# Values of a halo-attention layer: once per pixel through DRAM, in place of once per window

## The chip, the cores and the metric

The kernel runs on one core of a Trainium2 chip, as one program. The metric is the device time in microseconds, the median of several runs. The core has a matmul engine (TensorE, PE in the profile, with PEld for its loads of the stationary operand), a vector engine (DVE), a scalar engine (ACT), a general engine (POOL), a queue engine that issues most transfers (SP), and 16 DMA engines that all transfers share.

## What is computed

The input x is (2, 128, 256, 256) in fp32: two images of 128 channels. Two layers follow each other, each added to its input:

```
x = x + L0(groupnorm(x))        # halo attention
x = x + L1(groupnorm(x))        # convolutions
```

Layer 0, cut to what matters here:

```python
qkv = jnp.einsum('bchw,oc->bohw', x, W_qkv)
q, k, v = jnp.split(qkv, 3, axis=1)
q = ... # blocks of 8 x 8 pixels
k = unfold_windows(k)     # windows of 12 x 12 pixels, 8 apart: neighbours overlap by 4
v = unfold_windows(v)
attn = jnp.einsum('bnd,bmd->bnm', q * SCALE, k)          # 4 heads of 32
attn = attn + rel_pos_emb(q, rel_height, rel_width) + FIXED_MASK
out = jnp.einsum('bnm,bmd->bnd', softmax(attn), v)
out = ... # back to pixels
return jnp.einsum('bchw,oc->bohw', out, W_out)
```

The mask is minus infinity at every even relative row or column, so a query sees only keys of the other parity of row and of column. A block therefore falls into four classes of row parity r and column parity c, with 16 queries and 6 x 6 keys each. Layer 1 is a 5x1 convolution, a 3x1 depthwise one, a dilated 1x3 product with grouped weights, and their product. The change doesn't touch it.

## The kernel before

A strip is 8 rows of pixels, with its halo 12 rows. A unit u is a strip k and a row parity r, u = 2k + r; two images of 32 strips make 128 units. The normalised pixels of a strip lie in `xn[k % 2]`, a tile of [channel, row parity, column parity, XC = 131 columns j, 6 rows i]. One block needs 6 columns and neighbours start 4 apart, so with 6 rows in a column a pair of neighbouring blocks (10 columns, 60 keys, taken as 64) is one contiguous run, and the next pair starts 48 elements further. There are NPAIR = 16 pairs in a strip.

The values: keys must lie on partitions for the product with the attention weights, so the pixels of a pair are the stationary operand and the value weights stream past it. Every pair is done by itself; where the runs of two pairs overlap, the pixels are computed again. The two column parities fill the lower and the upper 64 partitions.

```python
vt = cst.tile([P, NPAIR, HEADS, 2, 33], F32, tag="f_vt", name="f_vt")   # 33rd column: ones
...
        def values(u, j):
            k, r = divmod(u, 2)
            xt = xn[k % 2].rearrange("p r c j i -> p r c (j i)")
            bank = []

            def part(n):
                if n == 0:
                    bank.append(ps_pj.tile([P, 512], F32, tag="pj", name=f"f_pv_{u}_{j}"))
                pv = bank[0]
                for c in range(2):
                    o = 48 * (4 * j + n)
                    nc.tensor.matmul(
                        pv[64 * c : 64 * c + 64, P * n : P * n + P], xt[:, r, c, o : o + 64], wvT,
                        start=True, stop=True,
                    )
                if n == 3:
                    for c in range(2):
                        rows = slice(64 * c, 64 * c + 64)
                        (nc.vector.tensor_copy if c else nc.scalar.copy)(
                            vt[rows, 4 * j : 4 * j + 4, :, c, 0:32],
                            pv[rows].rearrange("p (n h d) -> p n h d", n=4, h=HEADS),
                        )

            return [lambda n=n: part(n) for n in range(4)]
```

The vector engine and the scalar engine copy each bank into `vt`; the 33rd column of each head is 1 in the rows of its own column parity, so the sum of the attention weights comes out beside the product. `attend` uses `vt`:

```python
        def attend(u):
            p = pts.pop(u)
            on = wk.tile([P, 2, NPAIR, 32], F32, tag="on", name=f"f_on_{u}", bufs=1)
            k, r = divmod(u, 2)
            if r == 0:
                rcs[0] = wk.tile([P, 2, NPAIR, 2, 1], F32, tag="rc", name=f"f_rc_{k}")
            for lo, hi in ((0, 6), (6, 11), (11, NPAIR)):
                bank = ps_pj.tile([P, 512], F32, tag="pj", name=f"f_o_{u}_{lo}")
                po = bank[:, 0 : 66 * (hi - lo)].rearrange("p (n c d) -> p n c d", c=2, d=33)
                for n in range(lo, hi):
                    for h in range(HEADS):
                        nc.tensor.matmul(
                            po[32 * h : 32 * h + 32, n - lo], p[:, h, 32 * n : 32 * n + 32],
                            vt[:, n, h], start=True, stop=True,
                        )

                rc = rcs[0][:, r, lo:hi]
                nc.vector.reciprocal(rc, po[:, :, :, 32:33])
                nc.vector.tensor_tensor(
                    on[:, :, lo:hi].rearrange("p c n d -> p n c d"), po[:, :, :, 0:32],
                    rc.to_broadcast([P, hi - lo, 2, 32]), ALU.mult,
                )
        ...
```

The bias and score matmuls stand in `biases(u)` (line 360) and `scores(u, half)` (line 374), which end in the exponentials (line 382); the keys in `keys(u)` (line 278), the queries in `queries(u)` (line 297), the coefficients of the biases in `coefficients(k, t2)` (line 315), the output projection in `project(u)` (line 424), which adds the input rows and writes the result to DRAM. The order on TensorE is set by hand, on the other engines it is left to a scheduler:

```python
        load_rows(0)
        load_rows(1)
        with tc.manual_schedule(engines={PE}):
            normalise(0)
            emit(keys(0) + queries(0))
            for t2 in range(4):
                emit(coefficients(0, t2))
            for u in range(NU + 1):
                k, r = divmod(u, 2)
                b, s = divmod(k, NS)
                if u == NU:
                    project(u - 1)
                    break
                more = k + 1 < NB * NS
                if r == 0:
                    if k + 2 < NB * NS:
                        load_rows(k + 2)
                    if more:
                        normalise(k + 1)
                if b + 1 < NB and s + 1 < NS:
                    stats_chunk(b + 1, 2 * s + r)
                    if u < 2:
                        stats_chunk(b + 1, 2 * NS - 2 + u)

                biases(u)
                scores(u, 0)
                for j in range(4):
                    emit(values(u, j))
                scores(u, 1)
                if u + 1 < NU:
                    emit(keys(u + 1))
                if u > 0:
                    project(u - 1)
                attend(u)
                if more:
                    emit(coefficients(k + 1, 2 * r) + coefficients(k + 1, 2 * r + 1))
                if u + 1 < NU:
                    emit(queries(u + 1))
                del qs[u]
```

Rows are loaded by `load_rows(k)`, 10 rows of 256 pixels into a pool of four buffers, and normalised by `normalise(k)` (line 260); `stats_chunk` loads rows of the next image for its statistics (line 109). Ahead of all this the statistics of the first image are taken from 32 loads of 1 MB.

Of the kernel before, what the change touches and what calls it, by code (L numbers as in the profile page):

```python
# [9 lines left out]
F32 = mybir.dt.float32  # L10
# [8 lines left out]
P = 128  # L19
W = 256  # L20
HEADS = 4
# [118 lines left out]
        return mean, rstd  # L140


def attention_fast(tc, io, x1_d, norm, st_x, st_y, tags, ends):

    nc = tc.nc
    x = io["x"]
# [3 lines left out]
    with ExitStack() as l0:  # L150
# [34 lines left out]
        for c in range(2):  # L185
            nc.gpsimd.memset(vt[64 * c : 64 * c + 64, :, :, c, 32:33], 1.0)
        nc.gpsimd.memset(wb, 0.0)

        with ExitStack() as setup:
            sp = setup.enter_context(tc.tile_pool(name="f_setup", bufs=6))  # L190


            wq_nat = sp.tile([P, P], F32, tag="wq_nat", name="f_wq_nat", bufs=1)
            nc.sync.dma_start(wq_nat, io["w_q"])
            relT = sp.tile([P, 2 * NREL], F32, tag="relT", name="f_relT", bufs=1)
            nc.sync.dma_start(relT, io["relT"])
            g_rel = sp.tile([P, HEADS, 2 * NREL], F32, tag="g_rel", name="f_g_rel", bufs=1)
            for h in range(HEADS):
                pg = ps_pj.tile([P, 512], F32, tag="pj", name=f"f_pg_{h}")
                nc.tensor.matmul(  # L200
                    pg[:, : 2 * NREL], wq_nat[32 * h : 32 * h + 32, :],
                    relT[32 * h : 32 * h + 32, :], start=True, stop=True,
                )
# [123 lines left out]

            return [lambda t=t: part(t) for t in range(4)]

        def values(u, j):  # L330
            k, r = divmod(u, 2)
            xt = xn[k % 2].rearrange("p r c j i -> p r c (j i)")
            bank = []

            def part(n):
                if n == 0:
                    bank.append(ps_pj.tile([P, 512], F32, tag="pj", name=f"f_pv_{u}_{j}"))
                pv = bank[0]
                for c in range(2):
                    o = 48 * (4 * j + n)  # L340
                    nc.tensor.matmul(  # L341
                        pv[64 * c : 64 * c + 64, P * n : P * n + P], xt[:, r, c, o : o + 64], wvT,
                        start=True, stop=True,
                    )
                if n == 3:
                    for c in range(2):
                        rows = slice(64 * c, 64 * c + 64)
                        (nc.vector.tensor_copy if c else nc.scalar.copy)(  # L348
                            vt[rows, 4 * j : 4 * j + 4, :, c, 0:32],
                            pv[rows].rearrange("p (n h d) -> p n h d", n=4, h=HEADS),  # L350
                        )

            return [lambda n=n: part(n) for n in range(4)]

        def biases(u):
            k, r = divmod(u, 2)
# [27 lines left out]
        def attend(u):  # L384
# [9 lines left out]
                    for h in range(HEADS):  # L394
                        nc.tensor.matmul(  # L395
                            po[32 * h : 32 * h + 32, n - lo], p[:, h, 32 * n : 32 * n + 32],
                            vt[:, n, h], start=True, stop=True,
                        )

                rc = rcs[0][:, r, lo:hi]  # L400
# [209 lines left out]
def kernel_body(tc, io, out):  # L610
# [3 lines left out]
    with ExitStack() as ctx:  # L614
# [13 lines left out]
        attention_fast(tc, io, x1_d, norm, st_x, st_y, tags, ends)  # L628
# [572 lines left out]
```

## Time and profile before

| | |
|---|---|
| time, median of 3 | 4054.06 us (4048.38 to 4065.66) |
| span of the profiled run | 4070.9 us, mean granted TensorE clock 0.977 |
| first matmul of the first image's normalisation | 93.5 us |
| first and last bias matmuls of layer 0 | 111.5 us, 2645.8 us |
| matmuls of the values (line 341) | 8192 records, 521.0 us |
| their copies to `vt` (line 348) | DVE 512 x 694 ns, ACT 512 x 583 ns |
| DMA over the span | 362.10 MB, mean 89 GB/s |

A row of the profile's table of groups names the line, the engine, the operation, the tile written and the tiles read, the shapes, and the count, then the busy time in total, the mean of one, and the idle time of the engine ahead of it with what ended it. An fp32 matmul of the source appears as two records of TensorE, each with its load. The ends of matmuls are modelled: where one follows another, the distance of their starts says more than their length. In the 40 slices each digit is a tenth of the slice.

### The profile page before, as it was taken

What the parts mean: (1) busy time and instruction counts of PE and PEld (TensorE: products, weight loads), DVE (VectorE), ACT (ScalarE), POOL (GpSimd) and SP (SyncE); (2) the same over time, 40 slices, a digit from 0 to 9 for tenths busy, and PEclk for the clock granted to TensorE, in tenths of its full rate; (3) what the DMA queues carried; (4) which work ended last, traced back from release to release, by engine and by line L of the source; (5) the groups of instructions that cost most, each with busy time, mean ns of one, the idle gap of its engine ahead of it and who ended that gap; (6) DMA issues with size and microseconds to landing.
All of it is one profiled execution on the core that took longest, in us unless ns stands there. A gap on an engine that the chain in (4) does not pass through costs nothing. (4 is left out here: it accounts for less than half of the span.)

```text
span 4070.9 us, 144840 instructions
## 1 busy us (share of the span) xinstructions
PE 3641.6 (89%) x67638; PEld 2218.5 (54%) x67638; DVE 2272.4 (56%) x3377; ACT 1384.2 (34%) x2237; POOL 1084.9 (27%) x914
## 2 busy tenths in 40 slices
PE   0778988889989888988988989989999999999997
PEld 0556666666666666666666666643333334333333
DVE  8777656565655565656556565544444444444443
ACT  0333444444444444444444444422222222222221
POOL 1212222122222222212222122123333333333333
PEclk9999999999999999999999999989999999999998
DMA  9562212212212121221212211122222222222221
GB/s 377 190 198 81 68 60 68 68 55 68 72 56 65 55 68 55 73 68 55 68 55 73 68 55 65 34 92 104 97 90 104 104 93 96 101 103 104 90 97 70
DMA packets 71315, 362.10 MB, mean 89 GB/s; under 512 B 8496, under 2 KB 9136, under 8 KB 50224
## 3 DMA queue, kind: packets, MB, share of 16 engines
q1 hardware_dynamic: 43056, 218.49, 16.3%
q0 software_dynamic: 27648, 134.23, 8.4%
q8 instruction: 533, 8.73, 0.9%
q14 instruction: 78, 0.64, 0.1%
HBM read 218.48 MB, written 134.22 MB: 87 GB/s over the span
## 5 line engine op out<-in xcount | busy, mean ns | idle before, releaser
L570 PE MATMUL a<-xm,w 128*128 128x512 f32 (+1 forms) x2560 | 1129.8, 594 | 0.0
L570 PEld LDWEIGHTS a<-xm,w 128*128 128x128 f32 x2560 | 471.6, 188 | 654.5 <-issue 653.8
L589 DVE SCALAR_TENSOR_TENSOR t<-t,w,t 128x2048 f32<-128x2048 f32 x128 | 323.2, 2525 | 752.7 <-ACT t L574 752.6
L348 DVE COPY f_vt<-f_pv 64x512 f32<-64x512 f32 x512 | 354.1, 694 | 656.1 <-ACT f_vt L348 653.6
L348 ACT COPY f_vt<-f_pv 64x512 f32<-64x512 f32 x512 | 298.5, 583 | 756.2 <-PE f_pv L341 756.2
L341 PE MATMUL f_pv<-f_wqkvT,f_xn 128*64 128x128 f32 x8192 | 521.0, 286 | 29.6 <-issue 29.2
L374 PEld LDWEIGHTS f_s<-f_q,f_kt 32*64 32x64 f32 x32768 | 405.0, 134 | 194.0 <-issue 185.4
L374 PE MATMUL f_s<-f_q,f_kt 32*64 32x32 f32 x32768 | 411.6, 227 | 106.9 <-issue 106.6
L341 PEld LDWEIGHTS f_pv<-f_wqkvT,f_xn 128*64 128x64 f32 x8192 | 482.3, 144 | 43.1 <-issue 36.4
L574 ACT COPY t<-a 128x512 f32<-128x512 f32 (+1 forms) x256 | 149.6, 585 | 901.7 <-PE a L570 886.4
L268 POOL COPY f_xq<-f_xn 128x512 f32<-128x512 f32 x256 | 350.8, 1407 | 330.3 <-DVE f_xn L260 295.4
L321 ACT ACTIVATE f_cf<-f_pa,f_keep 128x256 f32<-128x256 f32 x256 | 207.1, 809 | 535.2 <-PE f_pa L315 534.5
L425 DVE TENSOR_TENSOR f_x<-f_py,f_raw 128x512 f32<-128x512 f32 x256 | 176.9, 693 | 263.3 <-PE f_py L424 260.7
L382 ACT ACTIVATE f_p<-f_s 128x512 f32<-128x512 f32 x512 | 265.4, 602 | 131.8 <-PE f_s L374 131.8
L286 POOL COPY f_kt<-f_kt 128x524 f32<-128x524 f32 x124 | 83.0, 669 | 841.5 <-ACT f_kt L281 841.5
L395 PEld LDWEIGHTS f_o<-f_vt,f_p 128*32 128x32 f32 x16384 | 241.4, 110 | 107.5 <-ACT f_kt L281 77.4
L315 PE MATMUL f_pa<-f_xq,f_wb 128*128 128x128 f32 x2048 | 276.5, 286 | 17.8 <-DVE f_on L402 14.6
L278 PE MATMUL f_pk<-f_xn,f_wqkvT 128*128 128x512 f32 (+1 forms) x528 | 277.0, 647 | 15.6 <-DVE f_vt L348 10.5
L395 PE MATMUL f_o<-f_vt,f_p 128*32 128x66 f32 x16384 | 263.6, 222 | 9.0 <-DVE f_x L425 9.0
L315 PEld LDWEIGHTS f_pa<-f_xq,f_wb 128*128 128x128 f32 x2048 | 248.7, 192 | 33.8 <-issue 14.7
L253 POOL COPY f_xn<-f_xn 128x1048 f32<-128x1048 f32 x62 | 71.1, 1146 | 732.2 <-PE f_pv L341 732.2
L424 PE MATMUL f_py<-f_ot,f_woT 128*128 128x512 f32 x512 | 246.3, 603 | 4.0 <-DVE f_ot L409 2.5
(103 smaller groups left out, 3601.4 us busy)
## 6 DMA issues: line engine op xcount, KB each, us to landing
f_raw<-in_x SPq DMA_DIRECT2D x62, 1280.0 KB, 7.0
f_x<-f_x POOLq DMA_DIRECT2D x128, 512.0 KB, 5.0
out<-y POOLq DMA_DIRECT2D x64, 1024.0 KB, 4.5
raw<-f_x SPq DMA_DIRECT2D x64, 640.0 KB, 4.2
f_sx<-in_x SPq DMA_DIRECT2D x32, 1024.0 KB, 12.4
f_sx<-in_x SPq DMA_DIRECT2D x64, 512.0 KB, 3.9
raw<-f_x SPq DMA_DIRECT2D x62, 384.0 KB, 4.7
f_raw<-in_x SPq DMA_DIRECT2D x2, 1024.0 KB, 5.6
```

The source lines that it names most:

```text
L268: nc.gpsimd.tensor_copy(xq[:, t2], by_place[:, t2])
L278: nc.tensor.matmul(pk[:, : n * P], wkT, xt[:, r, c, 1:129, lo:hi], start=True, stop=True)
L315: nc.tensor.matmul(pa[:, P * t1 : P * t1 + P], wb[:, t2, t1].rearrange("p h x -> p (h x)"), xq[:, t2, t1].rearrange("p a m -> p (a m)"), s ...
L321: nc.scalar.activation(cf[:, 0, t2], by_e[:, 0], AF.Identity, bias=keep[:, 1:2], scale=keep[:, 0:1])
L341: nc.tensor.matmul(pv[64 * c : 64 * c + 64, P * n : P * n + P], xt[:, r, c, o : o + 64], wvT, start=True, stop=True,)
L348: (nc.vector.tensor_copy if c else nc.scalar.copy)(vt[rows, 4 * j : 4 * j + 4, :, c, 0:32], pv[rows].rearrange("p (n h d) -> p n h d", n=4 ...
L374: nc.tensor.matmul(sc[h][64 * c : 64 * c + 64, 32 * n : 32 * n + 32], keys_k[rows, c, 48 * n : 48 * n + 64], qs[u][rows, c, 32 * n : 32 * ...
L382: nc.scalar.activation(pts[u][:, h], sc[h], AF.Exp)
L395: nc.tensor.matmul(po[32 * h : 32 * h + 32, n - lo], p[:, h, 32 * n : 32 * n + 32], vt[:, n, h], start=True, stop=True,)
L424: nc.tensor.matmul(py, woT, ots.pop((u, c)), start=True, stop=True)
L570: nc.tensor.matmul(pa[:, : n * W], w1[:, tap, :], xt[:, j - 2 + tap : j - 2 + tap + n, 2 : 2 + W], start=tap == 0, stop=tap == 4,)
L589: nc.vector.scalar_tensor_tensor(t3, t1[:, tap : tap + 8, :], w3[:, tap : tap + 1], t3, ALU.mult, ALU.add)
```

## The change

The values are computed once for every pixel. For a unit, each of the four new cells i of a column is a matmul of its own: 128 columns j of the pixel tile, 6 elements apart, are the stationary operand, and the values come out with columns on the partitions. One copy for each column parity takes a bank to `vx`, whose 33rd column holds ones from the start. From there a transfer writes them to a DRAM tile `v_d[r][k % 2]` of [column parity, 131 columns, 6 cells, 4 x 33], in which the order of memory is the order of keys; a second transfer writes the two cells that the next strip shares into that strip's tile. `gather(u)` then reads the 64 keys of every pair from DRAM into `vt`, one transfer for each column parity, 64 partitions by 16 pairs by 132 numbers. The edge columns of the DRAM tiles are filled once, with zeros and ones.

What this is for: the matmuls of the values use all 128 columns of the array, repeat nothing, and are copied out of PSUM in full height; the overlap is made by the transfers.

The values of unit u+1 are made in unit u, between the halves of the scores, and gathered after `attend(u)`. `vt` changes the order of its axes, with the column parity ahead of the head, and stays one tile with one buffer. The row loads move from the first unit of a strip to the second, and their pool goes from four buffers to three. Cut to its core:

```diff
-        vt = cst.tile([P, NPAIR, HEADS, 2, 33], F32, tag="f_vt", name="f_vt")
+        vt = cst.tile([P, NPAIR, 2, HEADS, 33], F32, tag="f_vt", name="f_vt")
+
+        vx = [cst.tile([P, 2, 4, HEADS, 33], F32, tag=f"f_vx{i}", name=f"f_vx{i}") for i in range(2)]
+        vx0 = cst.tile([P, 2, 2, HEADS, 33], F32, tag="f_vtop", name="f_vtop")
+
+        v_d = [
+            [dram.tile([2, XC, 6, HEADS * 33], F32, tag=f"f_v{r}{i}", name=f"f_v{r}{i}") for i in range(2)]
+            for r in range(2)
+        ]
...
         with ExitStack() as setup:
+            pad = ...tile([6, HEADS, 33], F32, tag="f_pad", name="f_pad")
+            nc.gpsimd.memset(pad, 0.0)
+            nc.gpsimd.memset(pad[:, :, 32:33], 1.0)
+            for r in range(2):
+                for i in range(2):
+                    for c in range(2):
+                        for j in (0, XC - 2, XC - 1):
+                            nc.sync.dma_start(v_d[r][i][c, j], pad.rearrange("p h d -> p (h d)"))
...
-        rawp = l0.enter_context(tc.tile_pool(name="f_raw", bufs=4))
+        rawp = l0.enter_context(tc.tile_pool(name="f_raw", bufs=3))
...
-        def values(u, j):
...
+        def values(u):
+
             k, r = divmod(u, 2)
...
+            s = k % NS
+            parts = [(0, vx0)] if s == 0 else []
+            for lo, t in parts + [(2, vx[u % 2])]:
+                n = 4 if lo else 2
+                banks = [ps_pj.tile([P, 512], F32, tag="pj", name=f"f_pv_{u}_{lo}_{c}") for c in range(2)]
                 for c in range(2):
...
+                    for i in range(n):
+                        nc.tensor.matmul(
+                            banks[c][:, P * i : P * i + P], xn[k % 2][:, r, c, 1:129, lo + i], wvT,
+                            start=True, stop=True,
                         )
...
+                    (nc.scalar.copy if c else nc.vector.tensor_copy)(
+                        t[:, c, :, :, 0:32],
+                        banks[c][:, : n * P].rearrange("p (i h d) -> p i h d", i=n, h=HEADS),
+                    )
+                nc.sync.dma_start(
+                    v_d[r][k % 2][:, 1:129, lo : lo + n].rearrange("c j i x -> j c (i x)"),
+                    t.rearrange("p c i h d -> p c (i h d)"),
+                )
+            if s + 1 < NS:
+                nc.sync.dma_start(
+                    v_d[r][(k + 1) % 2][:, 1:129, 0:2].rearrange("c j i x -> j c (i x)"),
+                    vx[u % 2][:, :, 2:4].rearrange("p c i h d -> p c (i h d)"),
+                )
+
+        def gather(u):
+
+            k, r = divmod(u, 2)
+            for c in range(2):
+                flat = v_d[r][k % 2][c].rearrange("j i x -> (j i) x")
+                src = bass.AP(
+                    tensor=flat.tensor, offset=flat.offset,
+                    ap=[[HEADS * 33, 64], [48 * HEADS * 33, NPAIR], [1, HEADS * 33]],
+                )
+                nc.sync.dma_start(
+                    vt[64 * c : 64 * c + 64, :, c].rearrange("p n h d -> p n (h d)"), src
+                )
...
-                            vt[:, n, h], start=True, stop=True,
+                            vt[:, n, :, h], start=True, stop=True,
...
             emit(keys(0) + queries(0))
+            values(0)
+            gather(0)
...
-                if r == 0:
-                    if k + 2 < NB * NS:
-                        load_rows(k + 2)
-                    if more:
-                        normalise(k + 1)
+                if r == 0 and more:
+                    normalise(k + 1)
+                if r == 1 and k + 2 < NB * NS:
+                    load_rows(k + 2)
...
                 scores(u, 0)
-                for j in range(4):
-                    emit(values(u, j))
+                if u + 1 < NU:
+                    values(u + 1)
                 scores(u, 1)
...
                 attend(u)
+                if u + 1 < NU:
+                    gather(u + 1)
```

More of the change, by code (lines that the diff above doesn't have):

```diff
@@ L140, in group, with attention_fast @@
         return mean, rstd
-def attention_fast(tc, io, x1_d, norm, st_x, st_y, tags, ends):
+def attention_fast(tc, io, x1_d, norm, st_x, st_y, tags, ends, dram):
     nc = tc.nc
@@ L184, in attention_fast @@
         nc.gpsimd.memset(vt, 0.0)
-        for c in range(2):
-            nc.gpsimd.memset(vt[64 * c : 64 * c + 64, :, :, c, 32:33], 1.0)
+        for i in range(2):
+            nc.gpsimd.memset(vx[i], 1.0)
+        nc.gpsimd.memset(vx0, 1.0)
         nc.gpsimd.memset(wb, 0.0)
         with ExitStack() as setup:
+            pad = setup.enter_context(tc.tile_pool(name="f_pad", bufs=1)).tile(
+                [6, HEADS, 33], F32, tag="f_pad", name="f_pad"
+            )
+            nc.gpsimd.memset(pad, 0.0)
+            nc.gpsimd.memset(pad[:, :, 32:33], 1.0)
+            for r in range(2):
+                for i in range(2):
+                    for c in range(2):
+                        for j in (0, XC - 2, XC - 1):
+                            nc.sync.dma_start(v_d[r][i][c, j], pad.rearrange("p h d -> p (h d)"))
             sp = setup.enter_context(tc.tile_pool(name="f_setup", bufs=6))
@@ L328, in coefficients @@
             return [lambda t=t: part(t) for t in range(4)]
-        def values(u, j):
+        def values(u):
             k, r = divmod(u, 2)
[L332 to L338, printed above, removed]
-                for c in range(2):
[L340 to L343, printed above, removed]
-                    )
[L345 to L353, printed above, removed]
+            s = k % NS
[3 more added lines that the diff above has]
+                banks = [ps_pj.tile([P, 512], F32, tag="pj", name=f"f_pv_{u}_{lo}_{c}") for c in range(2)]
+                for c in range(2):
+                    for i in range(n):
[6 more added lines that the diff above has]
+                        banks[c][:, : n * P].rearrange("p (i h d) -> p i h d", i=n, h=HEADS),
+                    )
+                nc.sync.dma_start(
[7 more added lines that the diff above has]
+                )
@@ new lines, in gather @@
+        def gather(u):
[8 more added lines that the diff above has]
+                    vt[64 * c : 64 * c + 64, :, c].rearrange("p n h d -> p n (h d)"), src
+                )
@@ L627, in kernel_body @@
         ends = glob.tile([P, NB * NS], F32, tag="f_ends", name="f_ends")
-        attention_fast(tc, io, x1_d, norm, st_x, st_y, tags, ends)
+        attention_fast(tc, io, x1_d, norm, st_x, st_y, tags, ends, dram)
         good = in_range(tc, glob, ends)
```

## The prediction

> **What bounds the kernel now.** I read the page first, for the busy shares and the 40 slices, then a table of busy time for the stretch of layer 0 alone, then TensorE's timeline over two units of layer 0, then what TensorE waited for there. The shares and slices of the page:
>
> ```profile
> PE 3641.6 (89%) x67638; PEld 2218.5 (54%) x67638; DVE 2272.4 (56%) x3377; ACT 1384.2 (34%) x2237; POOL 1084.9 (27%) x914
> ...
> PE   0778988889989888988988989989999999999997
> ...
> DMA  9562212212212121221212211122222222222221
> ```
>
> TensorE is the busiest engine from the third slice on. The change touches layer 0 alone: from 111.5 us (first bias matmuls) to 2645.8 us (last ones) the timeline counts 127 unit periods, so one of the 128 units takes 19.95 us on average. Busy time in that stretch:
>
> ```profile
> 104.00:2656.00 2552.00, 2256.02 (x62811) 1670.50 (x62810) 1564.07 (x2741) 1055.12 (x1797) 584.03 (x570) 0.97 0.22 73
> ```
>
> The columns are PE, PEld, DVE, ACT, POOL, granted clock, DMA share, GB/s. PE 88%, DVE 61%, ACT 41%, DMA 22%: TensorE bounds this stretch, the transfers have room. One unit on TensorE (start, length, engine, line, operation, count; brackets give idle time before it):
>
> ```profile
> 1023.23 1.12 PE L360 MATMUL f_s<-f_cf,f_hot 32*64 32x512 f32 x16 [1.48 <-DVE f_cf L324]
> 1024.14 1.53 PE L374 MATMUL f_s<-f_q,f_kt 32*64 32x32 f32 x128
> 1025.60 3.81 PE L341 MATMUL f_pv<-f_wqkvT,f_xn 128*64 128x128 f32 x64
> 1029.34 1.28 PE L374 MATMUL f_s<-f_q,f_kt 32*64 32x32 f32 x105
> 1031.35 0.43 PE L374 MATMUL f_s<-f_q,f_kt 32*64 32x32 f32 x23 [0.73 <-issue]
> 1031.71 2.02 PE L278 MATMUL f_pk<-f_xn,f_wqkvT 128*128 128x512 f32 x4
> 1033.58 1.88 PE L424 MATMUL f_py<-f_ot,f_woT 128*128 128x512 f32 x4
> 1035.38 2.05 PE L395 MATMUL f_o<-f_vt,f_p 128*32 128x66 f32 x128
> 1037.36 2.15 PE L315 MATMUL f_pa<-f_xq,f_wb 128*128 128x128 f32 x16
> 1039.34 1.88 PE L297 MATMUL f_pq<-f_xn,f_wq_s 128*128 128x512 f32 x4
> ```
>
> One source matmul in fp32 is two records. The values of line 341 occupy TensorE from 1025.60 to 1029.34, **3.74 us**; the coefficients of line 315, 16 records of a full 128x128 matmul with 128 moving columns, occupy 1037.36 to 1039.34, **1.98 us**. The shortest unit period on this timeline is 16.87 us, so on average 3.1 us of a unit are gaps and slower matmuls after gaps. The gaps:
>
> ```profile
> PE f_s L360 <- DVE f_cf L324: 115.2, 62, 2.9
> PE f_s L374 <- issue: 106.6, 77, 3.2
> PE f_pv L341 <- issue: 29.2, 33, 2.1
> PE f_pk L278 <- DVE f_vt L348: 10.5, 6, 4.8
> ```
>
> (waiter, releaser, total us, times, longest). Neither of the two large ones comes from the value computation; both should stay.
>
> [...] 110 ns for 32 columns (line 395), 137 for 64 (line 341), 192 for 128 (line 315), 0.85 ns a column. [...] The new stationary operand is a column of pixels 24 bytes apart; no load of the kernel before is strided, so this is untested here. [...] 512 B packets took 27 ns (median), 4096 B ones 159 ns, so 19 against 26 GB/s on one engine. [...]
>
> **The change part by part.**
>
> (1) Value matmuls. Now: 16 pairs x 2 column parities = 32 source matmuls a unit, 64 records, with overlapping 64-key windows: a key is computed 64/48 times, and each matmul uses half the columns. After: 2 parities x 4 row cells = 8 source matmuls, 16 records, each a full 128x128 by 128. That is the shape of line 315, whose 16 records take 1.98 us. Saved: 3.74 - 1.98 = 1.76 us a unit, all on the bounding engine: 128 x 1.76 = **225 us**. The first strip of each image adds 4 source matmuls for r = 0 and 1, about 1 us x 4 units = 4 us back. Net 221.
>
> (2) Evictions. Now 4 copies of 64x512 on DVE (4 x 694 ns) and 4 on ACT (4 x 583). After: one 128x512 copy on each (686 and 586 ns in comparable rows, lines 599 and 574). DVE gets 2.1 us a unit back, ACT 1.75. Most is beside TensorE and worth nothing, except in the first ten or so units: up to about 300 us, where the statistics of image 1 fill DVE to 77% and units take 24 to 29 us. There and in the waits on line 348 above I allow **15 us**.
>
> (3) Writes to DRAM. A unit writes 128 x 2 pieces of 2112 B (541 KB) and carries 128 x 2 of 1056 B (270 KB). They are issued in mid-unit, after the values, and must have landed before the next gather. From the end of the values to the end of attend there are second scores 1.5, keys 1.9, projection 1.8 and attend 2.0 = 7.2 us; a 512 KB transfer lands 3.9 to 5.0 us after issue in the page's table of issues. Hidden.
>
> (4) The gather. Two transfers of 64 x 16 pieces of 528 B, 541 KB each; 2048 pieces on 16 engines are 128 each, at 28 ns (scaled from the 27 ns of 512 B) 3.6 us. The page's transfers land 2.6 to 3.9 us later than such a sum (512 KB of row statistics: 8 packets x 0.16 = 1.3 against 3.9; rows of 1280 KB: 8 x 0.385 = 3.1 against 7.0). So both are in after 6.2 to 7.5 us. The values tile has one buffer: the gather for unit u+1 can start only when attend(u) has read it, and attend(u+1) needs it. Between lie coefficients 2.0, queries 1.8, biases 0.9, first scores 1.5, values 2.0, second scores 1.5, keys 1.9, projection 1.8 = **13.4 us** without gaps. The gather fits with 6 us to spare. Cost on the path: none.
>
> (5) DMA load. A unit moves 73 GB/s x 19.95 us = 1.46 MB now; 1.89 MB are added in about 18 us, near 185 GB/s. In the stretch 200 to 300 us the kernel already ran at 196 GB/s and a share of 0.60, and the idle time put to "issue" did not grow: 11.7 us between 110 and 300 us (6%) against 25.5 us between 1000 and 1500 us (5%). I allow 0.15 us a unit for contention, **20 us** back.
>
> (6) Set-up. Twenty-four small padding writes stand in the program ahead of the statistics loads and wait for memsets on POOL, which now end at 17.2 us and gain about 3. The statistics stage (first pm_x matmul at 93.5 us) is paced by DVE from its first load at 9.3 us on, so a late first load shifts everything: between 0 and 20 us according to the order in the queue. I put **10 us**. The prologue also gains values(0) and gather(0), largely under the coefficients: 3 us.
>
> (7) Row buffers from 4 to 3, loads one unit later. Rows for strip k+2 come into the buffer that the projection of unit 2k-1 frees, in unit 2k; the normalised rows are first wanted in unit 2k+3 for the values. More than a unit of slack: nothing.
>
> Sum: -221 - 15 + 20 + 10 + 3 = -203, so 4054 - 203 = **3851 us**, with a unit of about 18.3 us.
>
> **The rivals.** *A strided weight load costs the gain.* If every 24-byte step doubled the roughly 107 ns of a 128-column load (0.85 ns a column), 16 records would pace at some 215 ns instead of 124, values would take 3.4 us, and only 0.3 us a unit would be gained: about 4020 to 4040 us. [...] Against it: the queries already stream runs of 16 bytes at 24-byte pitch at 596 ns, as the contiguous line 570 does; and the normalisation on DVE reads elements 2 KB apart at a minimum of 889 ns for 1024 elements[...]. I give it 1 in 10, with half of it as likely again.
>
> *The gather becomes the wait.* If 528 B pieces take 100 ns and not 28, 128 of them take 12.8 us, plus some 3 us of latency: 16 us against 13.4, a wait of 2 to 3 us before each attend, time about 4150 to 4200. For it: more than 2000 small pieces in a burst[...], none like it in the kernel now. Against it: the 27 ns packets. 1 in 15.
>
> *Something else paces the unit.* Gaps put to "issue" in the scores could grow, as the values no longer give the sequencer 3.7 us with few instructions between two bursts of 256 records; or DVE's chain after attend (115 us of waits now) keeps units apart. If gaps take half of the gain, 3950.
>
> **Range and chances.** The chief term, 221 us, rests on two rows of one timeline; its likely errors (stride, issue gaps) lie on the slow side[...]. 8 in 10: 3785 to 3955 us. Faster by over 2% means under 3973 us: 0.87; within 2% 0.08; slower 0.05.
>
> **What would show it.** Right: values of 16 records in about 2.0 us on TensorE's timeline; unit period near 18.3 us; a gather that lands 6 to 8 us after issue; no row in which the attend matmuls wait for a DMA; DVE near 55% in layer 0. Wrong: weight loads of the values well over 192 ns (stride); attend released by the gather (transfer on the path); more than 250 us of "issue" gaps (fetching); first pm_x matmul later than 115 us (set-up).

## The result, and the profile after

The changed kernel takes **4188.01 us** (median of 4 runs, 4175.81 to 4190.53) against 4053.02 us before (now the median of 4 as well): ratio **1.0322**, 95% interval 1.0291 to 1.0353. It is slower. The prediction, 3851 us with a range of 3785 to 3955, was wrong, in its sign too.

The page after, busy shares and three rows of the 40 slices:

```profile
PE 3727.7 (89%) x61526; PEld 2267.4 (54%) x61526; DVE 1961.3 (47%) x2997; ACT 1167.3 (28%) x1857; POOL 1092.8 (26%) x917
...
PE   0888888988899989989888888989999999999997
...
PEclk9888898999998999999898888889999999999999
DMA  8888656666666566565656555542222222222221
```

TensorE has 6112 records fewer (67638 to 61526) and is busy for longer. DVE and ACT got their time back, to little use. New are a DMA share of 5 to 8 tenths in layer 0, and a granted clock that falls to 8 tenths in slices that showed 9 before. Layer 0 alone, columns as in the prediction:

```profile
127.50:2764.80 2637.30, 2325.23 (x56409) 1705.30 (x56409) 1245.12 (x2349) 831.91 (x1407) 580.88 (x562) 0.90 0.64 161
```

The clock was 0.97 there before and is 0.90, the DMA share went from 0.22 to 0.64. The two profiled spans differ by 117.8 us (4070.9 to 4188.7). The first bias matmuls start at 127.5 us in place of 111.5: 16 us of set-up. From there to the last ones layer 0 takes 2637.3 us in place of 2534.3: 103 us, or 0.81 us for each of 127 unit periods (20.77 against 19.95). What follows takes 1424 us in place of 1425. Layer 0 is where to look, and one stretch of TensorE's timeline shows its three features:

```profile
2315.49 1.37 PE L409 MATMUL f_s<-f_q,f_kt 32*64 32x32 f32 x115
2319.71 0.46 PE L409 MATMUL f_s<-f_q,f_kt 32*64 32x32 f32 x13 [2.85 <-issue]
2320.10 3.94 PE L359 MATMUL f_pv<-f_wqkvT,f_xn 128*128 128x128 f32 x16
2323.97 2.06 PE L409 MATMUL f_s<-f_q,f_kt 32*64 32x32 f32 x128
2325.95 3.65 PE L297 MATMUL f_pk<-f_xn,f_wqkvT 128*128 128x512 f32 x4
```

First, the 16 records of the values take 3.87 us from start to start, about as long as the 64 before, not the 1.98 us of line 334's equal shapes. Second, there is a gap of 2.85 us inside the first half of the scores, put to "issue": the last 13 records do nothing that the 115 ahead of them did not do. Third, the scores and keys that follow are slow (keys 3.65 us in place of 1.9), because the clock is at half after the gap: the trace's clock records show 0.5 from 2319.1 to 2329.3 us. "Issue" means that the engine waited for nothing that the profile shows. The waits of TensorE, before's lines 374, 360 and 341 being 409, 395 and 359 here:

```profile
PE f_s L409 <- issue: 172.6, 92, 4.0
...
PE f_s L395 <- DVE f_cf L343: 96.9, 63, 2.3
PE f_pv L359 <- issue: 32.0, 18, 3.4
```

"Issue" in the scores went from 106.6 to 172.6 us. No row of this view has the attend matmuls of line 430 waiting for a DMA: the gather is hidden, as predicted.

Where the unit's time went, summed over the timeline of layer 0 (stages by distance of starts without the gaps in brackets, per unit; half clock is the sum of the stretches that the trace's clock records show at 0.5):

| us a unit | before | after |
|---|---|---|
| values | 3.99 | 3.86 |
| scores | 3.08 | 3.30 |
| keys | 1.94 | 2.50 |
| other stages | 8.59 | 8.63 |
| gaps put to "issue" | 1.07 | 1.63 |
| gaps behind DVE f_cf | 0.92 | 0.75 |
| other gaps | 0.37 | 0.09 |
| half clock in the run, us | 187 | 558 |

The sum closes. Times 127 units the table gives -17 us for the values, +71 for the issue gaps, +99 for scores and keys, +5 for the other stages and -57 for the other two kinds of gaps; with 16 us of set-up and -1 after layer 0 that is 116 us, against 117.8 between the profiled spans. Scores and keys grew for the most part through half clock: at full clock a record of the keys takes 465 ns before and 464 after (means, from start to start), at half clock 861 and 876, and the share of key records at half clock went from 5% to 36%. A record of the scores takes 10.7 and 11.0 ns at full clock, 14.4 and 14.8 at half, and the share went from 5% to 21%.

**What the gaps are.** The page's queue q8 moves instructions, in packets of 16 KB, about 1.1 us each in the trace's packet records. The changed kernel has 485 of them, and 61526 matmuls with as many loads, 254 of these to a packet; before, 533 packets and 2 x 67638, also 254. So q8 carries TensorE's instructions. In layer 0 the kernel before has 66 gaps over 1 us that are put to "issue". Each of them has such a packet that ends in it or less than 1 us ahead of it, and TensorE resumes 1.39 us (median; 1.26 to 1.55 from the 10th to the 90th percentile) after the end of the packet. After the change it is all 86 of 86, and 1.45 us (1.28 to 1.64). In the stretch above the gap runs from 2316.86 to 2319.71 us and the packet from 2317.14 to 2318.44. So TensorE waits for its instructions. And the fetches go through the same engines as the data: when no fetch runs, the packet records of the kernel before mostly show 16 data packets in flight under load (602 us, against 70 us with 15 and 113 with 17), beside a fetch 15 (34 us, against 10 us with 14 and 6 with 16). A half of the scores is 256 instructions (128 matmuls, 128 loads) in 1.5 us, a packet's worth in little more than a packet's time. In the changed kernel 26 of the 86 packets start only after the gap has begun, before 4 of 66, and they take 1.33 us in place of 0.98 (medians).

### The profile page after: what moved, and what is told of

Same layout as the page of the kernel before. It is cut to its first block, busy times and chain, and to the rows that moved or that the text cites. A ratio compares the mean times of both kernels' runs of the same rounds, so it can differ in the third digit from the quotient of the medians.

```text
span 4188.7 us, 132486 instructions
## 1 busy us (share of the span) xinstructions
PE 3727.7 (89%) x61526; PEld 2267.4 (54%) x61526; DVE 1961.3 (47%) x2997; ACT 1167.3 (28%) x1857; POOL 1092.8 (26%) x917
## 5 line engine op out<-in xcount | busy, mean ns | idle before, releaser
L409 PE MATMUL f_s<-f_q,f_kt 32*64 32x32 f32 x32768 | 442.7, 238 | 172.7 <-issue 172.6
L409 PEld LDWEIGHTS f_s<-f_q,f_kt 32*64 32x64 f32 x32768 | 432.8, 146 | 261.2 <-issue 241.7
L359 PE MATMUL f_pv<-f_wqkvT,f_xn 128*128 128x128 f32 x2080 | 504.6, 408 | 34.7 <-issue 32.0
L359 PEld LDWEIGHTS f_pv<-f_wqkvT,f_xn 128*128 128x128 f32 x2080 | 474.9, 316 | 41.8 <-issue 35.9
L297 PE MATMUL f_pk<-f_xn,f_wqkvT 128*128 128x512 f32 (+1 forms) x528 | 343.8, 783 | 7.1 <-issue 6.8
L363 ACT COPY f_vx<-f_pv 128x512 f32<-128x512 f32 x128 | 75.0, 586 | 958.1 <-PE f_pv L359 935.6
L363 DVE COPY f_vx<-f_pv 128x512 f32<-128x512 f32 x128 | 88.9, 694 | 388.9 <-PE f_pv L359 388.6
L459 PE MATMUL f_py<-f_ot,f_woT 128*128 128x512 f32 x512 | 255.0, 622 | 2.1 <-DVE f_ot L444 2.1
L316 PE MATMUL f_pq<-f_xn,f_wq_s 128*128 128x512 f32 x512 | 242.8, 595 | 3.2 <-DVE f_on L437 2.4
```

What stands on the lines that cost most here:

```text
L297: nc.tensor.matmul(pk[:, : n * P], wkT, xt[:, r, c, 1:129, lo:hi], start=True, stop=True)
L316: nc.tensor.matmul(pq, wq_s, xn[k % 2][:, r, c, 1:129, 1:5], start=True, stop=True)
L359: nc.tensor.matmul(banks[c][:, P * i : P * i + P], xn[k % 2][:, r, c, 1:129, lo + i], wvT, start=True, stop=True,)
L409: nc.tensor.matmul(sc[h][64 * c : 64 * c + 64, 32 * n : 32 * n + 32], keys_k[rows, c, 48 * n : 48 * n + 64], qs[u][rows, c, 32 * n : 32 * ...
L459: nc.tensor.matmul(py, woT, ots.pop((u, c)), start=True, stop=True)
```

## The experiments

Theory A: the 24-byte pitch of the new stationary operand doubles its load, and the gain in the values is gone. Theory B: the transfers hold up the fetches of TensorE's instructions; longer gaps follow, and half clock after them. Rival C: the transfers cost only where something waits for their data. Half clock stands for stretches in which the trace's clock records show 0.5; a piece is one contiguous run of bytes of a transfer, one packet in the records. What a transfer puts on one DMA engine is an estimate, a sixteenth of its pieces: the page counts 16 engines, and the records don't name the engine of a packet. Each ratio is to the kernel before on the same chip. It took 4053 to 4083 us there (medians), so across groups of runs the ratios compare better than the times.

| run | ratio, 95% interval | time, us | values | issue gaps | half clock, us |
|---|---|---|---|---|---|
| change | 1.0322 (1.0291 to 1.0353) | 4188 | 3.86 | 1.63 | 558 |
| e1 contiguous operand | 1.0209 (1.0170 to 1.0249) | 4143 | 2.47 | 2.34 | 537 |
| e2 no transfers | 0.9742 (0.9714 to 0.9770) | 3963 | 3.83 | 0.56 | 258 |
| e3 both | 0.9417 (0.9390 to 0.9443) | 3831 | 2.26 | 0.85 | 223 |
| e5 before, with the transfers | 1.0627 (1.0589 to 1.0665) | 4331 | 4.48 | 1.80 | 476 |
| new layout | 1.0207 (1.0161 to 1.0253) | 4163 | 2.54 | 2.49 | 554 |
| e7 + gather in 8 | 0.9537 (0.9500 to 0.9573) | 3887 | 2.04 | 1.03 | 203 |
| e8 large pieces | 0.9635 (0.9599 to 0.9671) | 3933 | 2.48 | 1.31 | 350 |
| e9 change, gather in 8 | 0.9714 (0.9680 to 0.9748) | 3961 | 3.82 | 0.28 | 226 |
| e10 before, rows in 5 | 0.9839 (0.9809 to 0.9869) | 4011 | 3.90 | 0.77 | 164 |
| e11 rows issued by POOL | 0.9790 (0.9763 to 0.9818) | 3986 | 2.04 | 1.69 | 353 |
| e12 gather in 4 | 0.9970 (0.9951 to 0.9990) | 4055 | 2.42 | 1.79 | 452 |
| e13 e7 + rows in 5 | 0.9390 (0.9358 to 0.9422) | 3834 | 2.00 | 0.82 | 148 |
| e14 + 4 row buffers | **0.9317** (0.9291 to 0.9343) | 3801 | 2.03 | 0.90 | 141 |

(values and issue gaps in us a unit)

### Pitch and transfers, each alone and together

e1, the operand contiguous:

```diff
-   xn[k % 2][:, r, c, 1:129, lo + i], wvT,
+   xf[:, 6 + P * i : 6 + P * i + P], wvT,     # xf: the same tile, flat; other pixels
```

> The kernel after, but the stationary operand of each value matmul is a contiguous run of 128 numbers of the same pixel tile in place of 128 columns 24 bytes apart: other pixels, so the values are left wrong, with all counts, copies and transfers unchanged. Theory A (the 24-byte pitch doubles the load of the stationary operand): the load falls from 316 to about 192 ns, the value stage from 3.8 to 2.0 us a unit, and the time by 1.8 x 128 = 225 us to about 3960 us. Theory B (the transfers hold up the instruction fetch, and the gaps bring half clock; the pitch does not matter): loads stay near 316 ns and the time near 4188 us.

e2, no transfers:

```diff
-   nc.sync.dma_start(v_d[r][k % 2][...], t...)          # both writes
-   nc.sync.dma_start(vt[64 * c : 64 * c + 64, :, c]..., src)
+   nc.gpsimd.memset(vt[64 * c : 64 * c + 64, :, c, :, 32:33], 1.0)   # once, at the start
```

> The kernel after without the writes of the values to DRAM and without the gathers: the attention reads zeros and ones, the values are computed and copied but not used. Theory B: the gaps put to issue in the scores fall from 1.3 to 0.8 us a unit or less, half clock from 558 us to about 190 us, and the time by (0.55 + 0.78) x 128 = 170 us to about 4020 us. Theory A alone: value stage stays at 3.8 us, and nothing else changes: about 4180 us.

e3, both edits:

> Both edits together: contiguous stationary operand, no writes of the values and no gathers. If the two causes are independent and together are the whole: 4188 - 225 - 170 = about 3795 us, below the 3851 us predicted. If the gaps come from the shorter value stage or from something else, they stay above 1.3 us a unit and the time stays above 3900 us.

Measured: 4143, 3963 and 3831 us. Both causes are real: the value loads fall from 317 to 192 ns (median) with the contiguous operand, and the gaps from 1.63 to 0.56 us without transfers. The loads' row on the page of the change, then on that of e1 (316 and 225 ns are means):

```profile
L359 PEld LDWEIGHTS f_pv<-f_wqkvT,f_xn 128*128 128x128 f32 x2080 | 474.9, 316 | 41.8 <-issue 35.9
```

```profile
L360 PEld LDWEIGHTS f_pv<-f_wqkvT,f_xn 128*128 128x128 f32 x2080 | 294.8, 225 | 58.1 <-issue 52.7
```

TensorE's waits in e2:

```profile
PE f_s L403 <- issue: 68.3, 42, 2.8
```

But the two don't add. Beside the transfers the contiguous operand is worth 1.1 points of the ratio (1.0322 to 1.0209), without them 3.3 (0.9742 to 0.9417). In e1 the values are 1.39 us a unit shorter and the issue gaps 0.71 us longer: the scores come round sooner and wait longer for instructions. So theory A missed by 180 us in e1. Theory B was too small in e2: 5.8 points of the ratio fell away, some 236 us, not 170. In e2 the scores and keys are back at 3.04 and 1.98 us, so their growth came from the transfers too. The corner without both, 3831 us, comes close to the 3851 us that were predicted for transfers and a pitch that cost almost nothing.

### Which pitch costs

e4, the four value matmuls of a column parity on lines 359, 360, 362 and 363, at 4, 8, 16 and 24 bytes:

```diff
+   nc.tensor.matmul(banks[c][:, 0:P], xf[:, 6 : 6 + P], wvT, ...)
+   nc.tensor.matmul(banks[c][:, P : 2 * P], xf[:, 6 : 6 + 2 * P : 2], wvT, ...)
+   nc.tensor.matmul(banks[c][:, 2 * P : 3 * P], xf[:, 6 : 6 + 4 * P : 4], wvT, ...)
+   nc.tensor.matmul(banks[c][:, 3 * P : 4 * P], xf[:, 6 : 6 + 6 * P : 6], wvT, ...)
```

> The kernel after, the four value matmuls of a column parity on lines of their own, with stationary operands of 128 numbers at a pitch of 4, 8, 16 and 24 bytes (other pixels, values left wrong). [...] 4 and 8 bytes load in about 192 ns, 16 and 24 bytes in about 316 ns. If any pitch costs: 8 bytes is already at 316 ns. If the cost grows with the span: 8 bytes near 230, 16 near 270, 24 at 316 ns.

The instructions of the tile f_pv in the one execution of e4 (4159 us), with minimum, median and maximum in ns:

```profile
L359 PEld LDWEIGHTS f_pv<-f_wqkvT,f_xn x528: 186/189/338, 115.9 to 2719.0; 128*128 128x128 f32 x176
...
L360 PEld LDWEIGHTS f_pv<-f_wqkvT,f_xn x528: 192/198/338, 116.5 to 2719.2; 128*128 128x128 f32 x176
...
L362 PEld LDWEIGHTS f_pv<-f_wqkvT,f_xn x512: 308/329/333, 117.6 to 2719.5; 128*128 128x128 f32 x171
...
L363 PEld LDWEIGHTS f_pv<-f_wqkvT,f_xn x512: 296/318/321, 118.1 to 2720.0; 128*128 128x128 f32 x171
```

8 bytes load like 4 (198 and 189 ns, medians), 16 like 24 (329 and 318 ns). Among these four pitches the step is between 8 and 16 bytes; what makes it was not shown. The queries' moving operand, at 24-byte pitch but in runs of 16 bytes, takes 592 ns (median) in both kernels; a moving operand of single numbers at such a pitch was not tried.

### The transfers beside the kernel before

e5:

```diff
+   nc.vector.tensor_copy(vx[:, 0, 0, 0, 0:1], vt[...])      # holds the write to mid-unit
+   write(u + 1)                       # the two writes of the change, from a constant tile
...
+   nc.vector.tensor_tensor(junk, v2[...], on[...], ALU.add) # holds the gather behind attend
+   gather(u + 1)                      # the two gathers of the change, into the spare v2
```

> The kernel before, whole and with its own value matmuls, and beside it the transfers of the change on tiles that nothing else uses: the same writes from a constant tile in mid-unit, the same gathers of 2048 pieces after each attend, into a spare tile; three row buffers as in the change, and two one-element vector instructions a unit that hold the transfers to these places. A fill of 3.3 MB at the start adds some 10 us. Theory B (the transfers hold up the instruction fetch): gaps put to issue grow from 1.06 to 1.6 us a unit or more, half clock from 187 to about 500 us, and the time by 200 to 300 us to about 4280 us. Rival C (the transfers matter only where something waits for the gathered tile or for the value stage): the time stays near 4070 us.

Measured 4331 us, 6.3% slower than without, though no result depends on the transfers. The fill at the start matters less than expected: the first bias matmuls start at 114.3 us in place of 111.5. No wait of TensorE or of the vector engine in this run is put to the gathered tile, so rival C falls. TensorE's waits:

```profile
PE f_s L395 <- DVE f_cf L334: 168.2, 63, 3.0
PE f_s L409 <- issue: 120.1, 75, 4.0
PE f_pv L351 <- issue: 109.2, 44, 4.8
```

Issue gaps grow from 1.07 to 1.80 us a unit. Not all of it is theory B's: the waits for f_cf grow by 0.39 us a unit as well, some 50 us of the 257 by which the run is slower. The trace puts these to the probe itself. The added vector instruction that reads the spare tile takes 0.16 us (median), but 1.37 us in 49 of 128 units, and in each of these it ends together with a copy on POOL. In all 49 TensorE then waits for f_cf, 2.73 us (median) in place of 1.50 before.

### The layout that cures the pitch, and how a transfer is cut

The new layout stores row cells ahead of columns:

```diff
-   xn = [cst.tile([P, 2, 2, XC, 6], F32, ...) for i in range(2)]
+   xn = [cst.tile([P, 2, 2, 6, XC], F32, ...) for i in range(2)]
...
-   xn[k % 2][:, r, c, 1:129, lo + i], wvT,
+   xn[k % 2][:, r, c, lo + i, 1:129], wvT,
...
-   nc.scalar.copy(q[:, c, :], pq)
+   nc.scalar.copy(q[:, c, :].rearrange("p (j i) -> p i j", i=4), pq.rearrange("p (i j) -> p i j", i=4))
```

and the keys likewise.

> The kernel after with the pixel tile stored row cell first and column second, so that the 128 columns of a value matmul lie side by side; keys and queries come out in that order and are put back by their copies out of PSUM; nothing is left out. Theory A: value loads near 192 ns, value stage 2.0 to 2.5 us as in the run with the contiguous operand; theory B: the fetch gaps then grow to about 1.9 us a unit. Together about 4143 us, so still slower than before.

e7 cuts each gather by pairs, on this layout:

```diff
-   for c in range(2):      # 64 x 16 pieces
+   for g in range(0, NPAIR, 4):
+       for c in range(2):  # 64 x 4 pieces, vt[64 * c : 64 * c + 64, g : g + 4, c]
```

> The kernel with the new layout, each gather in four transfers of 4 pairs, so eight transfers a unit of 64 x 4 pieces: 16 pieces on each DMA engine in place of 64. If an instruction fetch waits until the share of one transfer on its engine is through (64 pieces of 49 ns are 3.1 us, 16 are 0.8 us): gaps fall from about 1.9 to 1.0 us a unit and the time to about 3950 us. If the fetch waits for all that is queued, or suffers from the load as such: no change, about 4143 us.

e12 does the same with `range(0, NPAIR, 8)`, four transfers a unit:

> The kernel with the new layout and each gather in two transfers of 8 pairs, four a unit: 32 pieces on each engine and transfer. Issues come 0.75 us apart, and 32 pieces take 0.9 us or more, so the engines don't run dry between transfers. If the share of one transfer counts: a share of half the size, gaps between 0.9 and 2.0, say 1.2 us a unit, and about 3950 us. If the eight transfers helped only because the slower issue leaves the engines idle in between: near the two transfers, about 4130 us.

e8 reads the same bytes in large pieces:

```diff
-   ap=[[HEADS * 33, 64], [48 * HEADS * 33, NPAIR], [1, HEADS * 33]]   # into vt
+   ap=[[1584, 64], [1, NPAIR * HEADS * 33]]                           # into a spare tile
```

> The kernel with the new layout, each gather replaced by a read of the same number of bytes from the same DRAM tile in 64 pieces of 8448 bytes into a spare tile; the attention reads zeros and ones, so its values are left out, and nothing waits for the gathers. If the number of small pieces does the harm: gaps fall to about 0.9 us a unit as without transfers, and the time to about 3880 us. If the bytes do it: about 4143 us.

The layout alone takes 4163 us, with a ratio like that of e1. With four transfers it is 4055, with eight **3887**, 276 us less than with two, for the same bytes and the same 2048 pieces a unit. TensorE's waits with two transfers, then with eight:

```profile
PE f_s L412 <- issue: 257.3, 141, 5.4
```

```profile
PE f_s L413 <- issue: 120.7, 82, 4.0
```

In this series the issue gaps follow the share that one transfer puts on one DMA engine: with 64 pieces they are 2.49 us a unit, with 32 pieces 1.79, with 16 pieces 1.03. Eight beat their expectation by 60 us; four landed between the expectation (3950) and its rival (4130). e8 lies between as well (1.31; 4 large pieces of 0.3 to 0.7 us on each engine and transfer). So neither the bytes nor the pieces of a unit are the measure. Nor is the share counted in time: 4 pieces of 0.61 us (median) are 2.4 us in e8, with smaller gaps than 32 pieces of 46 ns, 1.5 us, in e12. Why a fetch should wait for the share of one transfer, the traces don't show. One thing is mixed in: the eight issues take 6.2 us where two take 1.4 to 2.1, so the load is also thinner in time. The last packet of a gather ends no later with eight (8.6 us after the first issue, against 9.4, medians), but the 128 packets of an engine keep it busy for 3.6 us in place of 6.5 (28 and 51 ns each). That cutting the transfer helps is shown; by which of these ways is not.

e9, eight transfers on the change as it was:

```diff
-   for c in range(2):
+   for g in range(0, NPAIR, 4):
+       for c in range(2):
```

> The kernel after with its own pixel layout (24-byte pitch), and each gather in four transfers of 4 pairs, eight a unit; nothing left out. If the split removes most of what the transfers cost (225 us in this layout) and the pitch costs again what it costs without transfers (132 us): 3887 + 130, about 4015 us, value stage 3.8 us, gaps about 0.7 us a unit. If the split helps only together with the new layout: above 4100 us.

3961 us, 54 less than expected. This one edit turns the change from 3.2% slower into 2.9% faster than before, with the pitch still there: the values take 3.82 us, and the gaps nearly vanish (0.28). It is as fast as the change without any transfers (e2: 0.9742, with an interval that overlaps).

### Row loads

e10 edits the kernel before, and nothing else:

```diff
-   nc.sync.dma_start(t[:, 0:n, :], x[b, :, 8 * s : 8 * s + n, :])
+   for o in range(0, n, 2):
+       nc.sync.dma_start(t[:, o : o + 2, :], x[b, :, 8 * s + o : 8 * s + o + 2, :])
```

> The kernel before with each load of ten rows in five transfers of two rows: 8 pieces of 2 KB on each DMA engine in place of 8 of 10 KB (0.39 us each, 3.1 us in a row). If the share of one transfer on an engine is what holds up the fetches, and the row loads do so in the kernel before: gaps fall below 0.9 us a unit and the time by 20 to 60 us. If the gaps of the kernel before have nothing to do with its transfers: no change.

4011 us, 1.6% faster; gaps 0.77 in place of 1.07 us a unit. Thinner load is no explanation in this run: five issues take 3.21 us in the timeline at 1024.54 us, 0.64 each, and 8 packets of 84 ns keep an engine busy for 0.67, so it doesn't run dry. The gaps of the kernel before came in part from its own large transfers. The share of a transfer on an engine shrank in time, from 3.1 to 0.67 us, and stayed at 8 pieces, so a count of pieces is not the whole measure either.

e11 sends the row loads and the padding writes through POOL's queue:

```diff
-   nc.sync.dma_start(t[:, 0:n, :], x[b, :, 8 * s : 8 * s + n, :])
+   nc.gpsimd.dma_start(t[:, 0:n, :], x[b, :, 8 * s : 8 * s + n, :])
```

> The kernel with the new layout and the gathers in eight transfers, with the row loads and the padding writes issued by POOL in place of SP; nothing left out. Expected: the set-up no longer waits for POOL's memsets (first pm_x matmul back from 104 to about 94 us, 10 us), the 439 us for which the vector engine's normalisation waited for rows shrink; between 3850 and 3880 us. If the waits for rows were idle time that nobody needed: 3877 us.

The expectation failed: 3986 us, 100 more than e7. The set-up came back (first bias matmuls at 120.2 us in place of 124.4), and DVE's wait for rows shrank from 439 to 275 us, but the issue gaps rose to 1.69 us. In the timelines near 1000 us, e7 issues a row load (at 1020.44 us) behind its eight gathers, which SP issues there from 0.7 to 6.9 us after the start of the attend matmuls. In e11 POOL issues it 1.8 us after that start, and if SP issues the gathers as in e7, that is in their midst; that this is why the gaps grew was not shown.

e13 takes e7 with the row loads in five, on SP, and the padding writes on POOL; e14 adds the four row buffers and the early load of the kernel before:

```diff
-   rawp = l0.enter_context(tc.tile_pool(name="f_raw", bufs=3))
+   rawp = l0.enter_context(tc.tile_pool(name="f_raw", bufs=4))
...
-   if r == 1 and k + 2 < NB * NS:
+   if r == 0 and k + 2 < NB * NS:
```

> The kernel with the new layout and the gathers in eight transfers, with each row load in five transfers of two rows (on SP as before) and the padding writes issued by POOL; nothing left out. If the row loads are what still holds up the fetches: gaps fall from 0.93 to 0.5 us a unit, with the 10 us of set-up about 3820 us. If the rest of the gaps is the fetch's own: 10 us less than 3887, about 3877 us.

> As the run before it, with four row buffers and the row load in the first unit of a strip, as in the kernel before the change; nothing left out. If the late rows (the vector engine's normalisation waits for them, 439 us in the run with eight transfers) cost time on the path, through waits of the projection for the vector engine of 0.27 us a unit: 30 us less than the run before it. If nobody needs that time: the same.

3834 and **3801 us**: the best version is 6.8% faster than the kernel before (0.9317, 0.9291 to 0.9343), computes all of it, and moves the same bytes as the change. Layer 0 of e14:

```profile
113.20:2375.00 2261.80, 2031.05 (x56408) 1431.66 (x56408) 1201.84 (x2350) 1050.90 (x1407) 509.43 (x562) 0.98 0.64 188
```

The DMA share is 0.64 as in the change, but the clock 0.98 in place of 0.90. e13 gave 53 us against an expectation of 67, gaps 0.82 and not 0.5; 11 us of it are set-up (first bias matmuls at 113.3 us in place of 124.4). The step to e14 gave 33 us where 30 were expected; DVE's waits for rows, 379 us in e13, are no longer in the list.

## Why the prediction was wrong

- **Step 1, the value matmuls, failed**: 225 us were expected, 0.13 us x 128 = 17 us came. The 16 records pace at 239 ns at full clock (mean), not 124, with loads of 317 ns that are back at 192 with a contiguous operand (e1). The instruction count was right, the duration was taken from line 315, whose stationary operand is contiguous. The first rival had named the cause and the size of the stage (3.4 us against 3.9 measured) and got 1 chance in 10. Its two counterarguments were not about loads: one was a moving operand in runs of four numbers, the other a vector engine. A rival that no row refutes deserved more.
- **Step 5, contention, failed most**: 20 us were allowed; per unit the issue gaps grew by 0.56 us, and scores and keys by 0.78 us, which is 1.34 x 128 = 172 us. Without the transfers (e2) 5.8 points of the ratio fall away, some 236 us. The argument was that "issue" time did not grow between 110 and 300 us, where the DMA share was 0.60: 6% of the time against 5%. Per unit it did grow: 11.7 us over the 8 units that start there are 1.5 us each, 25.5 us over 26 units later on are 1.0. Units of 24 to 29 us hide that in a share of time. And the "issue" gaps of the kernel before were taken as a constant without asking what TensorE waited for; the packets of q8 would have told.
- **Step 4, the gather, was right in its verdict and wrong in a size**: attend waits for no DMA. The last packet of a gather ended 9.1 us (median) after the first issue, not 6.2 to 7.5, still inside the 13.4 us. A 528-byte packet took 49 ns (median), not 28; with the gathers in eight it took 28. The 27 ns packets were slower than the larger ones as well: 19 GB/s are three quarters of the 26 of the 4096 B packets, and 528 B in 49 ns are 11.
- **Step 2** was right as to sums. The first eight unit periods together fell from 211 to 185 us, but over the first sixteen the two kernels are even (366 and 365 us). Gaps other than "issue" fell from 1.29 to 0.84 us a unit. So there was some gain; that the evictions made it was not isolated.
- **Step 3**, the writes, showed no wait on the path.
- **Step 6**, set-up: 16 us to the first bias matmuls, 10 + 3 predicted; the first pm_x matmul came at 104.7 us.
- **Step 7**, row buffers, "nothing": DVE's normalisation waits 107 us for rows after the change. In the change itself the cost was not tried; between e13 and e14 it is 33 us.
- The second rival (the gather becomes the wait) did not happen. The third named the gaps in the scores, but as half of a gain, not as a loss greater than the gain. Its reason, that shorter values bring two bursts of instructions closer together, fits e1 (0.71 us a unit more); in the change itself the values were not shorter, and the transfers made the gaps.
- Of the signs of being wrong, the weight loads came (317 ns). More than 250 us of "issue" gaps did not: there were 207 us in layer 0, and much of the cost of the fetches came as half clock behind them.

## What to carry to other kernels

In this kernel TensorE's instructions come through the same 16 engines as the data (15 data packets in flight beside a fetch, 16 without one), and each of the 86 gaps over 1 us that are put to "issue" in the change goes with such a fetch. So before adding transfers to bursts of small matmuls, look for gaps inside a stage that nothing explains, and for the instruction queue's packets beside them. Transfers for which no engine waited still cost 257 us in e5, some 50 of them through the probe itself. Cutting the gathers so that one transfer puts about half a microsecond on an engine (by estimate, 16 pieces of 28 ns) gave back all that the transfers had cost in the change's own layout (0.9714 against 0.9742 without them), and most of it in the new one (0.9537, against 0.9417 without transfers and with a contiguous operand). And the duration of another row did not hold for another access pattern: a stationary operand with 16 or 24 bytes from column to column loaded in 329 and 318 ns, with 4 or 8 bytes in 189 and 198.

## What the runs showed of the hardware

- A load of the stationary operand took 110 ns (median) with 128 rows and 32 columns, 137 with 128 and 64, 192 with 128 and 128 (lines 395, 341 and 315 before), and 131 with 32 and 64, 182 with 32 and 128 (lines 360 and 596).
- Gaps of two to three microseconds on TensorE are mostly followed by stretches at half clock: within 7 us in 30 of 44 cases of layer 0 before the change, in 53 of 54 after it. For gaps of 1.0 to 1.5 us it was 5 of 66 and 27 of 70. The clock records show these stretches in steps of 3.4 us (127.7 to 131.2, 134.6 to 141.4 us in the changed kernel). Through them 0.56 us of added gaps came with 0.78 us more in scores and keys.
- The value matmuls at 24-byte pitch pace at 239 ns a record at full clock and at 237 at half, those of the kernel before at 59 and 107 (means): half clock cost the strided values nothing.
- ACT's copies of keys into the new layout's order, 24 bytes from element to element, took 1102 ns in place of 644 (medians), and the normalisation on DVE, which now reads neighbours 8 bytes apart and not 2 KB, 811 ns in place of 1315. ACT was busy for 832 us of layer 0 in the change and for 1051 in e14, of more than 2200.
- SP's queue was held (medians) for 0.76 us by a gather of 1024 pieces in the change and for 0.61 by one of 256 pieces in e7, but for 0.37 by a write of 256 pieces and for 0.35 by a row load of 128.
